# Four-layer attention kernel on one core: the last feed-forward and the final attention placed in other, fewer ticks

## The chip, the core and the metric

The kernel runs on one core of a Trainium2 chip. A core has a matrix engine (TensorE; PE in the profile, its weight loads PEld), a vector engine (VectorE, DVE), a scalar engine for activations (ScalarE, ACT), a general one (GpSimd, POOL) and a sync engine (SP) that issues the DMAs. Each engine works through its own instructions in order; semaphores hold an instruction until what it needs is done. The metric is the device time of one execution in microseconds; the median of several runs counts.

## The reference

`x` is 8 batches of 256 rows by 128, `ctx_512` is 8 batches of 64 rows by 64. Four blocks follow one another:

```python
x = L0(x, ctx_512)      # attention to the context, 16 heads, gate, layer norm
x = L1(x, ctx_512)      # attention to the context, one head, residual
x = L2(ctx_512, x, ...) # six decoder layers: self attention, cross attention, feed-forward
x = L3(x, ctx_512)      # the final attention
```

One decoder layer of L2, and L3, where the change lies:

```python
def step(t, p):
    tn = _ln(t, norm_g, norm_b)
    t = _mha(tn, tn, skv, sq, sow, sob, tgt_mask) + t      # 16 heads of 64
    tn = _ln(t, norm_g, norm_b)
    t = _mha(src, tn, ckv, cq, cow, cob, src_mask) + t
    tn = _ln(t, pg, pb)
    return t + (relu(tn @ w1 + b1) @ w2 + b2)              # 128 -> 512 -> 128

def L3(emb, latent, Wq, bq, Wk, bk, Wv, bv, gamma, beta):
    q = emb @ Wq + bq
    k, v = latent @ Wk + bk, latent @ Wv + bv
    w = softmax(q @ k.T / sqrt(128), axis=1)               # over the 256 rows, not the 64 keys
    x = w @ v + emb
    return layernorm(x, eps=1e-6) * gamma + beta
```

The softmax of L3 runs over the 256 rows of `emb`. The kernel holds the weights with the 64 keys on the partitions, sums along the row, and so can divide the 64 rows of `v` by the sums instead of the weights.

## The kernel before

All activations stay on chip in the tile `t`, 128 rows by 16 blocks by 128 (two blocks a batch). The work is cut into steps of one batch (or half a batch), and every step is put into a table by hand: `at(tick, phase, fn)`. At the end the table is walked tick by tick, and within a tick by phase; each step's instructions are chained behind those before them on the same engine (PE, DVE, ACT, POOL; SP's queue follows the order in which the DMAs are issued). So the table alone sets each engine's order. A tick has no length of its own: it is only the place of a step in the queues, and a step that waits holds everything behind it on that engine.

In the rest of the text, ticks are counted from the first cross-attention tick of the last layer (`T_ca` of layer 5 is tick 0). Batch `b` of the last layer's cross attention has its scores in ticks 2b and 2b+1 (`sc`, L341 and L348, then L357 on ACT, L359 on DVE, L360 on POOL, and L366 on ACT at phase 8), divides a tick later (L370 and L371 on DVE, L372 on POOL), transposes another tick later (L380 on DVE), and sums with the values (L388 on PE, phase 3.0, and L1104 on DVE) in ticks 2b+3 and 2b+4. The last scores stand in tick 15 and the last sums in tick 18. The values of the cross attention (L303) and, for every second batch, its keys (L1079) are made in even ticks.

`plan_ff` places the feed-forward of a batch: the statistics of the normalisation (`moments`, L808 and L809 on DVE; `scales`, L814 to L821 on POOL), the normalisation (L827, ACT), its transpose (L841 on PE, L843 on ACT), `first` (L1120 on PE, L1125 Relu on ACT, the residual L290 on POOL) and `second` (L1137 on PE, L1141 on DVE, which writes `t`).

`plan_l3` places the final attention in five steps, one a tick:

- `trans`: two transposes of `t` (L1158, PE) and a copy (L1160, ACT).
- `project`: queries and values (L1164, L1165 on PE; L1169, L1173 on DVE).
- `weights`: scores (L1177, PE), maximum (L1179, DVE), exponential with its sum (L1182, ACT).
- `values`: reciprocal of the sum (L1186, DVE) and scaling of `v` (L1187, DVE), the product (L1190, PE), the residual (L1195, DVE), the statistics (L262, L263 on DVE; L265, L267 on POOL).
- `finish`: the normalisation (L1201, DVE), scale and shift (L1205, L1206 on POOL) and the store (L1207, SP).

`keys_l3` makes the keys of all batches of L3 once (L407 on PE, L416 on DVE). Its tile shares its place (tag `AT`, one buffer) with the folded keys of the layer before, which are read last in tick 10.

The steps of the last layer in ticks, with the phase in brackets:

| step | batches 0 to 5 | batch 6 | batch 7 |
|---|---|---|---|
| moments, scales | 2b+4 (6, 8.4) | 16 (6, 8.4) | 18 (6, 8.4) |
| normalisation | 2b+5 (3.3) | 17 (3.3) | 19 (3.3) |
| its transpose | 2b+6 (2.9) | 18 (2.9) | 20 (2.9) |
| first | 2b+7 (3.1) | 19 (3.1) | 21 (3.1) |
| second | 2b+8 (3.2) | 20 (3.2) | 22 (3.2) |
| trans | 2b+9 (4.5) | 21 (4.5) | 23 (4.5) |
| project | 2b+10 (4.4) | 22 (4.4) | 24 (4.4) |
| weights | 2b+11 (4.3) | 23 (4.3) | 25 (4.3) |
| values | 2b+12 (4.2) | 24 (4.2) | 26 (4.2) |
| finish | 2b+13 (4.1) | 25 (4.1) | 27 (4.1) |

The keys of L3 are made in tick 11 (3.9).

Of the kernel before, what the change touches and what calls it, by code (L numbers as in the profile page):

```python
# [12 lines left out]
ALU = mybir.AluOpType  # L13
# [4 lines left out]
B, S, D = 8, 256, 128  # L18
M, DM = 64, 64
NL, H, HD, FF = 6, 16, 64, 512  # L20
# [7 lines left out]
def tile_xattn_stack(ctx: ExitStack, tc: tile.TileContext, io, out: bass.AP):  # L28
    nc = tc.nc
# [31 lines left out]
    def sb(shape, tag, bufs=2, pool=None):  # L61
        return (pool or act).tile(shape, F32, tag=tag, name=uniq(tag), bufs=bufs)
# [216 lines left out]
    def at(tick, phase, fn):  # L279
        plan.setdefault(tick, []).append((phase, fn))  # L280
# [121 lines left out]
    S0 = {}  # L402
# [399 lines left out]
    def ahead(b, stats_at, normal_at, tT_at, g, bias, st, on_scalar=True):  # L802

        def moments():
            st["mv"] = sm([P, QT, 2], "mv")
            for j in range(QT):
                six = sm([P, 6], "six")
                nc.vector.bn_stats(six, tt(b)[:, j, :])  # L808
                nc.vector.bn_aggr(st["mv"][:, j, :], six)  # L809

        def scales():
            mv = st["mv"]
            ve = sm([P, QT], "ve")
            nc.gpsimd.tensor_scalar(ve, mv[:, :, 1], 1e-5, None, ALU.add)  # L814
            st["rstd"] = sm([P, QT], "rstd")
            nc.gpsimd.tensor_tensor(st["rstd"], ve, mhalf, ALU.pow)
            if on_scalar:
                nm = sm([P, QT], "nm")
                nc.gpsimd.tensor_tensor(nm, mv[:, :, 0], st["rstd"], ALU.mult)
                st["nm"] = sm([P, QT], "nm2")  # L820
                nc.gpsimd.tensor_scalar(st["nm"], nm, -1.0, None, ALU.mult)  # L821

        def normal():
            st["xn"] = sb([P, QT, D], "xn", 3)
            for j in range(QT):
                if on_scalar:
                    nc.scalar.activation(  # L827
                        st["xn"][:, j, :], tt(b)[:, j, :], AF.Identity,
                        scale=st["rstd"][:, j : j + 1], bias=st["nm"][:, j : j + 1],
                    )  # L830
                else:
                    nc.vector.tensor_scalar(
                        st["xn"][:, j, :], tt(b)[:, j, :], st["mv"][:, j, 0:1],
                        st["rstd"][:, j : j + 1], ALU.subtract, ALU.mult,
                    )

        def trans():
            ps = tp_tile()
            xn = st.pop("xn")
            for j in range(QT):  # L840
                nc.tensor.transpose(ps[:, j * P : (j + 1) * P], xn[:, j, :], ident)  # L841
            st["tT"] = sb([D, S], "tT", 5)
            nc.scalar.activation(st["tT"], ps[:, :S], AF.Identity, scale=g, bias=bias)  # L843

        at(*stats_at, moments)
        at(stats_at[0], 8.4, scales)
        at(*normal_at, normal)
        at(*tT_at, trans)
# [260 lines left out]
                nm2[:, b].unsqueeze(1).to_broadcast([P, 4, M]), lambda ps, qt=qt: add(qt, ps),  # L1109
            )  # L1110

    def plan_ff(l, b, T, T_second):
        st = {}

        def first():
            w1 = W["ff", l][0]
            hT = big("o", shape=(P, FF // P, S))
            ps = two_banks("mm")
            for c in range(FF // P):
                nc.tensor.matmul(  # L1120
                    ps[:, c * S : (c + 1) * S], lhsT=w1[:, c * P : (c + 1) * P], rhs=st["tT"],
                    start=True, stop=True,
                )
            for c in range(FF // P):
                nc.scalar.activation(  # L1125
                    hT[:, c, :], ps[:, c * S : (c + 1) * S], AF.Relu, bias=ff_b1[:, l, c : c + 1]
                )
            st["hT"] = hT
            st["tb"] = residual(b, W["ff", l][2])

        def second():
            w2 = W["ff", l][1]
            ps = mm_tile()
            hT = st.pop("hT")
            for j in range(QT):
                for c in range(FF // P):
                    nc.tensor.matmul(  # L1137
                        ps[:, j * D : (j + 1) * D], lhsT=hT[:, c, j * P : (j + 1) * P],
                        rhs=w2[:, c, :], start=(c == 0), stop=(c == FF // P - 1),
                    )  # L1140
            nc.vector.tensor_add(  # L1141
                tt(b), ps[:, :S].rearrange("p (a d) -> p a d", a=QT), st["tb"]
            )

        ahead(b, (T - 3, 6), (T - 2, 3.3), (T - 1, 2.9), pre_g[:, l : l + 1], pre_b[:, l : l + 1], st)
        at(T, 3.1, first)
        at(T_second, 3.2, second)

    out_v = out.rearrange("b (j p) d -> b p j d", p=P)
# [1 line left out]
    def plan_l3(b, T):  # L1151

        st = {}

        def trans():
            ps = tp_tile()
            for j in range(QT):
                nc.tensor.transpose(ps[:, j * P : (j + 1) * P], tt(b)[:, j, :], ident)  # L1158
            st["tT"] = sb([D, S], "tT", 5)
            nc.scalar.copy(st["tT"], ps[:, :S])  # L1160

        def project():
            ps = mm_tile()
            nc.tensor.matmul(ps[:, :S], lhsT=w3q, rhs=st.pop("tT"), start=True, stop=True)  # L1164
            nc.tensor.matmul(  # L1165
                ps[:M, S : S + D], lhsT=ctx2[:DM, b], rhs=w3v, start=True, stop=True
            )
            st["q"] = sb([D, S], "q1")
            nc.vector.tensor_scalar(  # L1169
                st["q"], ps[:, :S], b3q, float(D) ** -0.5, ALU.add, ALU.mult  # L1170
            )
            st["v"] = sb([M, D], "v1")
            nc.vector.tensor_add(st["v"], ps[:M, S : S + D], b3v)  # L1173

        def weights():
            sc = mm_tile()
            nc.tensor.matmul(sc[:M, :S], lhsT=S0["k3T"][:, b], rhs=st.pop("q"), start=True, stop=True)  # L1177
            nm = sm([M, 1], "nm3")
            nc.vector.tensor_reduce(nm, sc[:M, :S], AX.X, ALU.max, negate=True)  # L1179
            st["e"] = sb([M, S], "tT", 5)  # L1180
            st["rs"] = sm([M, 1], "rs3")
            nc.scalar.activation(st["e"], sc[:M, :S], AF.Exp, bias=nm, accum_out=st["rs"])  # L1182

        def values():
            v, rs = st.pop("v"), st.pop("rs")
            nc.vector.reciprocal(rs, rs)  # L1186
            nc.vector.tensor_scalar(v, v, rs, None, ALU.mult)  # L1187
            ps = mm_tile()
            for j in range(QT):
                nc.tensor.matmul(  # L1190
                    ps[:, j * D : (j + 1) * D], lhsT=st["e"][:, j * P : (j + 1) * P], rhs=v,
                    start=True, stop=True,
                )
            y = st["y"] = sb([P, QT, D], "y")
            nc.vector.tensor_add(y, ps[:, :S].rearrange("p (a d) -> p a d", a=QT), tt(b))  # L1195
            st["norm"] = stats(y, 1e-6)

        def finish():
            y, (mv, rstd) = st.pop("y"), st.pop("norm")
            for j in range(QT):  # L1200
                nc.vector.tensor_scalar(  # L1201
                    y[:, j, :], y[:, j, :], mv[:, j, 0:1], rstd[:, j : j + 1],
                    ALU.subtract, ALU.mult,
                )
            nc.gpsimd.tensor_tensor(y, y, ln3_g.unsqueeze(1).to_broadcast([P, QT, D]), ALU.mult)  # L1205
            nc.gpsimd.tensor_tensor(y, y, ln3_b.unsqueeze(1).to_broadcast([P, QT, D]), ALU.add)  # L1206
            nc.sync.dma_start(out=out_v[b], in_=y)  # L1207

        for n, step in enumerate((trans, project, weights, values, finish)):
            at(T + n, 4.5 - 0.1 * n, step)  # L1210


    at(0, -1, lambda: load_sa(0))
# [3 lines left out]
    for b in range(B):  # L1217
        plan_l0(b, 2 * b)
        plan_l1(b, 2 * b + 7)
    T0 = 2 * B + 1  # L1220
    for l in range(NL):
        T_ca = T0 + 4 * B
        T_next = T_ca + 2 * B
        for b in range(B):
            plan_sa(l, b, T0 + 4 * b)
        plan_ca_weights(l, T_ca - 6)
        for b in range(B):
            plan_ca(l, b, T_ca + 2 * b)
            T_ff = T_ca + 2 * b + 7
            plan_ff(l, b, T_ff, T_ff + (2 if l + 1 < NL else 1))  # L1230
        if l > 0:
            at(T0 + 8, -1, lambda l=l: load_ff(l))
        if l + 1 < NL:
            at(T_ca + 4, -1, lambda l=l: load_sa(l + 1))
            at(T_next + 1, -1, lambda l=l: load_ca(l + 1))
        T0 = T_next
    def keys_l3():
        S0["k3T"] = sb([D, B, M], "AT", 1, heap)
        keys(w3k, S0["k3T"], b3k)

    at(T_ca + 11, 3.9, keys_l3)
    for b in range(B):
        plan_l3(b, T_ca + 2 * b + 9)

    engines = (
        mybir.EngineType.PE, mybir.EngineType.DVE, mybir.EngineType.Activation,
# [72 lines left out]
```

## Time and profile before

| | |
|---|---|
| median of 3 runs | 2443.6 us (2442.93 to 2445.48) |
| the profiled execution's own time | 2442.87 us |
| its span in the profile | 2441.1 us |
| granted clock of PE, mean of the span | 0.987 |
| busy share of the span | PE 96%, PEld 71%, DVE 75%, ACT 70%, POOL 59% |
| chain that ended last | PE 77%, DVE 8%, ACT 7%, POOL 5%, issue 2% |
| start of L388 in ticks 11 to 18 (us from the span's start) | 2331.7, 2341.4, 2351.2, 2359.2, 2373.6, 2379.9, 2388.9, 2397.7 |

The span runs from the first to the last event of the profile; the execution's own time holds 1.8 us more. "Busy" is the time in which an engine has an instruction in work. The timeline gives an instruction's start, its duration, and in brackets how long the engine was idle before it and what ended that. "A <- B: 5.3, 3, 2.4" in the list of waits reads: A waited for B, 5.3 us in all, three times, 2.4 us the longest. The windows view gives for each stretch its length, then the busy time of each engine with the number of instructions, the granted clock of PE, the DMA share and GB/s. Times in the text are from the span's start.

### The profile page before, as it was taken

The numbers are of one execution on the slowest core, as the hardware profiler recorded it, in microseconds if no ns is written. First come the engines' busy times: TensorE is split into PE (matmuls) and PEld (weight loads), VectorE is DVE, ScalarE is ACT, GpSimd is POOL, SyncE is SP. The second block draws the span as 40 slices with busy tenths as digits, with TensorE's granted clock in tenths as the row PEclk, the third lists the DMA queues.
The fourth block names the chain that finished last, engine by engine and source line by source line (L and its number), as shares of the span: only waits on it lengthen the run. The fifth ranks groups of instructions, "written<-read, shape, count | busy, mean of one in ns | idle before, by whom it ended". The sixth has DMA issues, their size and how long they took to land.

```text
span 2441.1 us, 99984 instructions
## 1 busy us (share of the span) xinstructions
PE 2349.7 (96%) x42411; PEld 1742.3 (71%) x42411; DVE 1839.3 (75%) x5988; ACT 1718.1 (70%) x4528; POOL 1450.2 (59%) x2483
## 2 busy tenths in 40 slices
PE   8999999999999999999999999999999999999986
PEld 4667777777777677777777777777777777777764
DVE  5778887677887667887767887667888667888664
ACT  5577777677777667777667777667777667778642
POOL 4845557754556755556855556755556765555763
PEclk9999999999999999999999999999999999999998
DMA  6000022000022001022001022001012000010000
GB/s 177 2 11 14 23 75 57 2 12 21 20 72 64 2 3 30 20 72 64 2 3 30 20 63 64 11 3 30 20 55 72 12 2 26 24 53 5 2 3 16
DMA packets 102833, 76.88 MB, mean 31 GB/s; under 512 B 8113, under 2 KB 96881, under 8 KB 102386
## 3 DMA queue, kind: packets, MB, share of 16 engines
q1 hardware_dynamic: 101794, 70.16, 10.4%
q8 instruction: 334, 5.47, 0.9%
q14 instruction: 113, 0.93, 0.1%
q10 hardware_dynamic: 592, 0.33, 0.1%
HBM read 62.07 MB, written 8.39 MB: 29 GB/s over the span
## 4 chain that ended last, share of the span: by engine, by line
PE 77%; DVE 8%; ACT 7%; POOL 5%; issue 2%; DMA 0%; SPq 0%; POOLq 0%; DVEq 0%; ACTq 0%
PE mm L861 14%; PE sc L898 14%; PE mm L953 13%; PE mm L971 7%; PE mm L880 7%; PE mm L388 5%; PE sc L341 4%; PE mm L1120 3%; PE mm L1137 2%; DVE m L359 2%; ACT e L357 2%; POOL e L360 2%; PE mm L1079 2%; PE tp L841 1%; PE mm L303 1%
## 5 line engine op out<-in xcount | busy, mean ns | idle before, releaser
L927 POOL TENSOR_SCALAR e<-e,rs 128x256 f32<-128x256 f32 x1536 | 703.0, 478 | 673.3 <-DVE rs L925 664.0
L917 ACT ACTIVATE e<-e,mn 128x256 f32<-128x256 f32 x1536 | 758.2, 495 | 133.8 <-DVE mn L912 129.5
L912 DVE CUSTOM_DVE_ANT_0 e<-sc,nm 128x256 f32<-128x256 f32 x1536 | 542.4, 419 | 107.7 <-PE sc L898 106.2
L937 DVE STREAM_TRANSPOSE eTc<-e 128x512 f32<-128x512 f32 x768 | 517.3, 695 | 62.5 <-POOL e L927 61.2
L898 PE MATMUL sc<-k,q 64*32 64x256 f32 x12288 | 377.7, 380 | 1.9 <-ACT v L286 1.0
L953 PE MATMUL mm<-eTc,v 32*64 32x256 f32 x12288 | 363.9, 377 | 5.7 <-ACT AT L1054 3.3
L953 PEld LDWEIGHTS mm<-eTc,v 32*64 32x64 f32 x12288 | 277.3, 131 | 88.7 <-issue 22.7
L359 DVE TENSOR_REDUCE m<-sc 128x16 f32<-128x1024 f32 x112 | 136.7, 1221 | 269.2 <-ACT e L357 269.2
L360 POOL TENSOR_TENSOR e<-e,m 128x1024 f32<-128x1024 f32 x112 | 213.1, 1902 | 209.8 <-DVE m L359 209.8
L898 PEld LDWEIGHTS sc<-k,q 64*32 64x32 f32 x12288 | 221.3, 106 | 122.2 <-issue 48.9
L917 ACT ACTIVATION_READ_ACCUMULATOR e<-e,mn 128x1 f32 x1536 | 287.1, 187 | 0.0
L341 PE MATMUL sc<-q,tT 128*32 128x256 f32 x3072 | 222.0, 388 | 3.0 <-DVE t L1104 2.3
L372 POOL TENSOR_TENSOR e<-e,r 128x1024 f32<-128x1024 f32 x112 | 213.0, 1902 | 2.9 <-DVE r L371 2.9
L388 PE MATMUL mm<-v,o 128*128 128x128 f32 x1536 | 202.2, 287 | 0.0
L388 PEld LDWEIGHTS mm<-v,o 128*128 128x128 f32 x1536 | 188.9, 201 | 16.1 <-issue 8.7
L861 PE MATMUL mm<-tT,w_sk 128*128 128x256 f32 x768 | 189.1, 389 | 0.0
L971 PEld LDWEIGHTS mm<-w_sow,o 128*128 128x128 f32 x1536 | 175.1, 192 | 17.0 <-issue 12.3
L880 PE MATMUL mm<-w_sv,tT 128*32 128x256 f32 x3072 | 185.7, 382 | 0.0
L286 ACT COPY v<-mm 128x1024 f32<-128x1024 f32 x96 | 97.2, 1012 | 124.3 <-PE mm L880 123.7
L971 PE MATMUL mm<-w_sow,o 128*128 128x128 f32 x1536 | 183.6, 278 | 0.8 <-ACT WVO L1052 0.8
L861 PE MATMUL mm<-tT,w_sq 128*128 128x256 f32 x768 | 173.6, 379 | 0.0
L861 PEld LDWEIGHTS mm<-tT,w_sk 128*128 128x128 f32 x768 | 138.1, 190 | 44.1 <-issue 29.2
(212 smaller groups left out, 3544.5 us busy)
## 6 DMA issues: line engine op xcount, KB each, us to landing
nm<-mask_d SPq DMA_DIRECT2D x192, 128.0 KB
wd<-o SPq DMA_DIRECT2D x48, 128.0 KB
w_sk<-in_L_sa_kv_dram SPq DMA_DIRECT2D x6, 512.0 KB
w_sv<-in_L_sa_kv_dram SPq DMA_DIRECT2D x24, 128.0 KB
w_sq<-in_L_sa_q_dram SPq DMA_DIRECT2D x6, 512.0 KB
w_sow<-in_L_sa_ow_dram SPq DMA_DIRECT2D x6, 512.0 KB
w_ckv<-in_L_ca_kv_dram SPq DMA_DIRECT2D x12, 256.0 KB
w_cq<-in_L_ca_q_dram SPq DMA_DIRECT2D x6, 512.0 KB
```

Of the source, the lines that this page charges most:

```text
L341: nc.tensor.matmul(sc[32 * a : 32 * a + 32, q, :], lhsT=qT()[:, qb * 32 : (qb + 1) * 32], rhs=keys()[:, a].rearrange("p h k -> p (h k)"), ...
L360: nc.gpsimd.tensor_tensor(e, e, m.unsqueeze(2).to_broadcast([P, 16, M]), ALU.subtract)
L388: nc.tensor.matmul(ps[:, :D], lhsT=eT[:, s].rearrange("p q x -> p (q x)"), rhs=vw[:, r, k, g, :], start=(s == 0), stop=(s == 7),)
L861: nc.tensor.matmul(ps[:, i * S : (i + 1) * S], lhsT=w[:, c * P : (c + 1) * P], rhs=st["tT"], start=True, stop=True,)
L880: nc.tensor.matmul(ps[32 * a : 32 * a + 32, i, :], lhsT=st["tT"][:, kb * 32 : (kb + 1) * 32], rhs=sv[:, a].rearrange("p g x -> p (g x)"), ...
L898: nc.tensor.matmul(sc[32 * a : 32 * a + 32, r, j, :], lhsT=st["q"][g][rows, a, qb * 32 : (qb + 1) * 32], rhs=st["k"][g][rows, a, :], start ...
L912: nc.vector.tensor_tensor_reduce(e[:, i, :], sc4[:, i, :], st["nm"][:, 2 * jj + i % 2, :], -1.0, 3.0 * BIG, ALU.add, ALU.min, mn[:, i : i ...
L917: nc.scalar.activation(e[:, i, :], e[:, i, :], AF.Exp, scale=-1.0, bias=mn[:, i : i + 1], accum_out=rs[:, i : i + 1],)
L927: nc.gpsimd.tensor_scalar(e[:, i, :], e[:, i, :], rs[:, i : i + 1], 1.0, ALU.mult, ALU.mult)
L937: nc.vector.transpose(eT[:, r, :, 2 * jj : 2 * jj + 2, :], e[:, 2 * r : 2 * r + 2, :].rearrange("p j (k x) -> p k j x", x=32),)
L953: nc.tensor.matmul(ops[a // 2][r * HD : (r + 1) * HD, a % 2, :S], lhsT=st["v"][kb // 4][rows, kb % 4, (2 * g + r) * HD : (2 * g + r + 1) * ...
L971: nc.tensor.matmul(st["ps"][:, j * D : (j + 1) * D], lhsT=st["oT"][c // 4][:, c % 4, j * P : (j + 1) * P], rhs=sow[:, c, :], start=(c == 0 ...
```

## The change

Three things are moved; no instruction is added or left out.

- The feed-forward of the last layer for batches 6 and 7 takes other ticks.
- The final attention begins in the tick behind `second` at phase 0.5, that is at the tick's head; `project` follows in the same tick at 4.5, `weights` one tick later, and the division of `v` becomes a step of its own at the end of that tick (8.6); `values` and `finish` follow one and two ticks behind.
- The keys of L3 are made in tick 6 instead of 11, in a buffer of the ring `k`, which the cross attention of the last layer does not use.

The new places:

| step | batches 0 to 5 | batch 6 | batch 7 |
|---|---|---|---|
| moments, scales | 2b+4 (6, 8.4) | 16 (6, 8.4) | 18 (6, 8.4) |
| normalisation | 2b+5 (3.3) | 16 (8.7) | 18 (8.7) |
| its transpose | 2b+6 (2.9) | 18 (2.9) | 19 (2.9) |
| first | 2b+7 (3.1) | 18 (4.6) | 19 (4.6) |
| second | 2b+8 (3.2) | 19 (3.2) | 20 (3.2) |
| trans, project | 2b+9 (0.5, 4.5) | 20 (0.5, 4.5) | 21 (0.5, 4.5) |
| weights, divide | 2b+10 (4.3, 8.6) | 21 (4.3, 8.6) | 22 (4.3, 8.6) |
| values | 2b+11 (4.2) | 22 (4.2) | 23 (4.2) |
| finish | 2b+12 (4.1) | 23 (4.1) | 24 (4.1) |

The diff, cut to its core:

```diff
-    def plan_ff(l, b, T, T_second):
+    def plan_ff(l, b, T, T_second, steps=None):
...
-        ahead(b, (T - 3, 6), (T - 2, 3.3), (T - 1, 2.9), pre_g[:, l : l + 1], pre_b[:, l : l + 1], st)
-        at(T, 3.1, first)
+        first_at, *steps = steps or (3.1, (T - 3, 6), (T - 2, 3.3), (T - 1, 2.9))
+        ahead(b, *steps, pre_g[:, l : l + 1], pre_b[:, l : l + 1], st)
+        at(T, first_at, first)
         at(T_second, 3.2, second)
...
+        def divide():
+            rs = st.pop("rs")
+            nc.vector.reciprocal(rs, rs)
+            nc.vector.tensor_scalar(st["v"], st["v"], rs, None, ALU.mult)
+
         def values():
-            v, rs = st.pop("v"), st.pop("rs")
-            nc.vector.reciprocal(rs, rs)
-            nc.vector.tensor_scalar(v, v, rs, None, ALU.mult)
+            v = st.pop("v")
...
-        for n, step in enumerate((trans, project, weights, values, finish)):
-            at(T + n, 4.5 - 0.1 * n, step)
+        at(T, 0.5, trans)
+        at(T, 4.5, project)
+        at(T + 1, 4.3, weights)
+        at(T + 1, 8.6, divide)
+        at(T + 2, 4.2, values)
+        at(T + 3, 4.1, finish)
...
-            plan_ff(l, b, T_ff, T_ff + (2 if l + 1 < NL else 1))
+            if l + 1 < NL:
+                plan_ff(l, b, T_ff, T_ff + 2)
+            elif b < B - 2:
+                plan_ff(l, b, T_ff, T_ff + 1)
+            else:
+                T_ff -= b - B + 3
+                done = T_ca + 2 * b + 4
+                plan_ff(
+                    l, b, T_ff, T_ff + 1,
+                    (4.6, (done, 6), (done, 8.7), (T_ff, 2.9)),
+                )
+            T_end[b] = T_ff + 1
...
-        S0["k3T"] = sb([D, B, M], "AT", 1, heap)
+        S0["k3T"] = big("k", shape=(D, B, 2 * M))[:, :, :M]
         keys(w3k, S0["k3T"], b3k)
 
-    at(T_ca + 11, 3.9, keys_l3)
+    at(T_ca + 6, 3.9, keys_l3)
     for b in range(B):
-        plan_l3(b, T_ca + 2 * b + 9)
+        plan_l3(b, T_end[b] + 1)
```

From `plan_l3` on the changed file has other line numbers (the copy L1160 is L1161 there, the product L1190 is L1194, the normalisation L1201 is L1205); the prediction names lines by the numbers of before.

More of the change, by code (lines that the diff above doesn't have):

```diff
@@ L1220, in tile_xattn_stack @@
     T0 = 2 * B + 1
+    T_end = {}
     for l in range(NL):
```

## The prediction

> **What bounds the kernel now.** I read the page first, then windows and PE's waits over the last 110 us, the chain of waits there, and the timeline. PE is busy 96% of the span and carries 77% of the chain, so time is won only where PE stands or runs slowly, and behind its last large group. The windows view of the stretch that the change touches:
>
> ```profile
> 2341.36:2359.17 17.81, 16.00 (x201) 11.59 (x199) 13.76 (x29) 7.52 (x15) 12.05 (x14) 1.00 0.01 2
> 2359.17:2379.91 20.74, 17.17 (x152) 11.57 (x151) 12.92 (x28) 7.78 (x13) 11.23 (x13) 0.84 0.02 7
> 2397.67:2441.10 43.43, 25.75 (x133) 17.84 (x132) 17.90 (x65) 8.06 (x26) 14.54 (x26) 0.81 0.05 16
> ```
>
> Stretch, length, busy time of PE, PEld, DVE, ACT, POOL, granted clock. Two ticks take 17.8 us with PE busy 16.0, or 20.7 at clock 0.84; behind the last sums (L388, 2397.67) PE is busy 25.75 of 43.4 us. PE's waits from 2331 to 2398, and after 2397.67 (us in all, times, longest):
>
> ```profile
> PE mm L1190 <- DVE v L1187: 5.3, 3, 2.4
> PE tp L841 <- ACT xn L827: 2.2, 2, 1.1
> PE mm L1177 <- DVE AT L416: 1.1, 1, 1.1
> PE sc L341 <- ACT o L1125: 0.7, 1, 0.7
> ...
> PE mm L1190 <- DVE v L1187: 7.3, 5, 2.1
> ```
>
> The first row is the wait for the division: step values stands ahead of the next tick's scores in PE's order, and its L1187 is last in DVE's, behind L1141. The chain of waits (start, us) shows why DVE is late there:
>
> ```profile
> 2356.28 1.87 DVE y L1201 x2
> 2358.15 0.34 DVE nm L1179
> 2358.51 0.56 ACT tT L1182 x2
> 2359.07 0.26 ACT tT L1160
> 2359.33 0.96 ACT e L366
> ...
> 2365.18 0.33 DVE t L1141
> 2365.61 0.76 DVE v L1187
> 2366.41 1.02 PE mm L1190 x4
> ```
>
> In the odd tick output, softmax and copy of the last attention stand ahead of L366, 3.0 us that come out at L1190. What follows such a wait, in windows of 3.41 us:
>
> ```profile
> 2363.26:2366.67 3.41, 0.98 (x34) 0.44 (x16) 3.02 (x8) 1.97 (x2) 3.02 (x2) 1.00 0.00 0
> 2366.67:2370.08 3.41, 3.41 (x20) 1.72 (x23) 2.11 (x8) 0.00 (x0) 1.08 (x3) 0.50 0.00 0
> 2383.74:2387.15 3.41, 1.59 (x37) 0.90 (x24) 2.54 (x8) 1.01 (x1) 1.90 (x1) 1.00 0.00 0
> 2387.15:2390.56 3.41, 3.41 (x13) 2.43 (x13) 2.79 (x12) 0.00 (x0) 1.64 (x4) 0.50 0.00 0
> ```
>
> After PE was busy 0.98 or 1.59 of 3.41 us the clock is 0.50, both times for two windows; at it L388 took 3.78 us (2388.85) against 1.95 (2397.67).
>
> **Part 1: the ticks up to the last sums (2331.7 to 2397.7).** I count ticks from the last layer's first cross-attention tick; L388 of tick 18 starts at 2397.67.
>
> Removed: PE's four waits above, 9.3 us. The first goes because the division now ends a tick (8.6), one tick before values: DVE does it (0.14 and 0.28 to 0.75 us) ahead of L359, which alone is queued behind it and waits 1.1 to 4.0 us for L357 in odd ticks anyway; without that cover it costs its 0.9 a batch, on DVE. The third goes since the keys are built five ticks early; their 1.1 us of PE and 0.7 of DVE move, at nothing (bounds -1.1 and +1.1). The other two are waits of the next tick's first matmuls for ACT (Relu L1125, then the normalisation L827 behind it). Before them PE did weights and trans at the end of an odd tick (0.95 us); now it does values and project there (0.6 + 1.0), 0.65 more cover: the 0.7 becomes 0.1, the 1.1 before L841 becomes 0.4 in tick 16; in tick 18 it goes, since batch 6 is now normalised at the end of tick 16.
>
> Added: trans is now first in a tick (0.5), ahead of all scores, and needs L1141 of the tick before. L1141 ended 0.2 us after L303 at 2346, 1.5 at 2365.5, 1.2 at 2385.9. Weights (0.6) now lies between, and the 3.0 us above leave the odd tick, so I take 0 there and 0.14 of issue each, 0.4; tick 9, with neither, adds 0.9 (L303 ends 2312.1, L1141 2312.9). No row shows the new order: bounds 0 and 2.4 each (the longest L1190 wait). With the 0.5 left above, 1.8 stay. Project and values of one batch more are done by the last sums: +1.6. So -9.3 + 1.8 + 1.6 = -5.9.
>
> Clock: without windows half empty the slow stretches go. L1190, L1164, L1165 and the scores took 2.7 + 4.4 us from 2366.4, against 1.6 (from 2347.2) and 2.3 (from 2356.6): 3.2. L1164, L1165, L388, L1120 took 7.9 from 2387.1, against 1.0 + 1.8 + 1.8: 3.3. Together -6.5.
>
> At nothing, with their cover: POOL's four ops of an output (2.4 us) and its store come a tick sooner; POOL is busy 12.05 of 17.8, and SP's queue holds only such stores then. The two L1201 (1.95 us beside a POOL op, 0.6 alone) and L1179 go to even ticks, where the next tick's first user of DVE's late results is L388, behind scores. L1160 moves ahead of L357 on ACT: 0.25 us, ACT being busy 7.5 of 17.8. If this cover fails each costs its length once a batch.
>
> On the clock the Trainium skill speaks against this change. "TensorE: Matmul & The Clock Gate", section "Why this matters for your kernels", asks only that PE not idle over about 3 us between bursts. By it waits of 2.4 us cost no clock, and their removal wins none. The trace disagrees: 2.4 and 1.8 us idle, and the clock fell.
>
> **Part 2: the drain (2397.67 to 2441.1, 43.4 us).** Of batches 6 and 7 the feed-forward's first product moves from ticks 19 and 21 to 18 and 19, the second from 20 and 22 to 19 and 20; the last attention ends in tick 24 instead of 27. PE's new order from the last sums, at full-clock durations (L388, L1137, L1120 1.8; L1177, L1190 0.6; L1164 with L1165 1.0; trans 0.4): L388, L1137 of batch 5, weights of 4, L1120 of 6, trans of 5: 6.4. Then L841 of batch 7 needs its statistics, whose POOL part stands behind output 3 and a residual: L1201 done 5.0, L1205 and L1206 1.5, L290 0.7, L814 to L821 1.5, L827 to L841 0.6 (timeline): 9.3, a new wait of 2.9 with all of PE behind it. L841, L1137 of 6, values of 4, project of 5, L1120 of 7, trans of 6 end at 15.2; L1137 of 7 waits 0.3 for Relu and ends at 17.3. Three softmaxes follow one another, each 3.1 from L1177 to L1190 (2423.51 to 2426.64), with L1190 between: 17.3 + 3.1 + 0.6 + 3.1 + 0.6 + 3.1 + 0.7 = 28.5. From L1190's end (2433.48) to the span's end: 7.6, so 36.1. Output 7 uses the buffer of output 5, stored at about 26 and landed within 2.9 (last issue 2438.24 to the span's end): 0 to 0.8, I take 0.4. So 36.5 against 43.4: -6.9.
>
> New clock losses: the 2.9 us wait can empty a window, 3.3 as above; the softmaxes leave PE mostly idle, and a second fall costs like that at 2404 (L1120 3.6 against 1.8): 1.7. I take both, +5.0 (bounds 0 and 8.3).
>
> **Sum.** -5.9 - 6.5 - 6.9 + 5.0 = -14.3. The profiled execution took 2442.87 (span 2441.1 and 1.8 around it), 0.7 under the median 2443.6: 2429.3, so 2429.
>
> **Rivals.**
>
> The falls have another cause than the waits. They come as often as before: no 6.5, no 5.0, and the 1.8 at 2404 stays: -5.9 - 6.9 + 1.8 = -11.0, 2432.6. For it: the fall at 2404 came behind a window with PE busy 2.36 of 3.41 us. Against: the two costly ones came behind 0.98 and 1.59. The Trainium skill's rule above would lead here.
>
> Small waits suffice. After 2400.80 PE was busy 2.36 of 3.41 us, and 0.50 followed; so the waits at trans keep the 6.5: -5.9 - 6.9 + 5.0 = -7.8, 2435.8. Against: 2.27 and 2.35 (2407.63, 2411.04) were not followed by it.
>
> The ticks are bound by the loop scores, L357, L359 to L1104 (8 us), whatever PE waits for. DVE's 13.8 of 17.8 speak for it, the 14 us of two earlier ticks (L388 at 2300.5 and 2314.4) against. Then -6.9 + 5.0 = -1.9, 2441.7, no change.
>
> Slower: trans at the tick's head, six times (ticks 9 to 19), has all scores behind it. It decides when L1141 ends later than 0.6 + 1.7 us after L303, half a window empty: six waits of 1.7 are 10.2, a fall in every second pair 9.9, less 1.3 counted, and the 6.5 not won: -14.3 + 18.8 + 6.5 = +11.0, 2454.6. Against: 0.2 to 1.5 us in the rows.
>
> That it does not do what it says: the plan chains each engine's instructions by tick and phase, so only a buffer could hold a step, and those are counted.
>
> **How the numbers follow.** Forecast 0.62, other cause 0.13, small waits 0.14, loop 0.05, slower 0.06. Low end: without new clock losses, trans waits and the keys' 1.1, -14.3 - 5.0 - 1.3 - 1.1 = -21.7, 2421. High end: 2435.8 and one trans wait at its bound, 2438. Outside lie the last two rivals and some of the forecast's tails. 0.2% of the median is 4.9 us, about what a measurement of this kernel can tell from no change. Faster by more: 0.89; within: 0.05; slower: 0.06.
>
> **What would show it.** Right: no PE wait for the division in ticks 12 to 17, waits of trans for L1141 under 1 us, granted clock 1.00 until the last sums, these near 2385; nearly 3 us of wait before the last L841; 36 to 42 us from the last sums to the end. Wrong: clock 0.50 in those ticks (the clock rivals), trans waiting over 1.7 us (slower), last sums after 2392 with PE idle elsewhere (loop).

## The result, and the profile after

The changed kernel takes 2433.9 us (median of 5 runs, 2430.0 to 2435.6) against 2444.7 for the kernel before beside it (5 runs): ratio 0.9953, 95% interval 0.9938 to 0.9967, so the medians lie 10.8 us apart, and the ratio says 0.47%, with an interval from 8 to 15 us. The forecast of 2429 was 4.9 us too low; the range held the time.

The profiled execution of after has a span of 2431.9 us. Its start-up and the layers ahead, where both programs are the same, came out 6.4 us later than in the profile of before, so whole spans mislead here. I compare one stretch instead: from the first L388 of tick 6 (2291.87 before, 2298.24 after) to the end of the span. It took 149.3 us before (the expectations say 149.0) and 133.7 after, 15.6 less, where the forecast's sum was 14.3.

The windows view of after, the columns being stretch, length, busy time of PE, PEld, DVE, ACT, POOL, granted clock, DMA share and GB/s: ticks 12 and 13, ticks 14 and 15, and from the last sums to the end.

```profile
2347.89:2363.84 15.95, 15.92 (x200) 11.61 (x199) 12.64 (x29) 8.68 (x17) 12.61 (x14) 1.00 0.04 10
2363.84:2378.14 14.30, 13.84 (x152) 10.30 (x151) 11.81 (x26) 7.55 (x15) 10.96 (x12) 1.00 0.04 10
2389.69:2431.94 42.25, 26.98 (x126) 19.74 (x124) 15.75 (x59) 8.25 (x23) 14.57 (x26) 0.72 0.05 16
```

In the ticks PE is busy 15.92 of 15.95 us and 13.84 of 14.30, at full clock; before, the same two pairs took 17.81 and 20.74. Behind the last sums nearly nothing changed: 42.25 us for 43.43, at a clock of 0.72 for 0.81. PE's waits from 2300 to 2432 (us in all, times, longest):

```profile
PE mm L1194 <- DVE v L1188: 4.4, 3, 2.0
PE tp L841 <- ACT xn L827: 3.3, 2, 2.9
PE tp L1159 <- DVE t L1141: 0.8, 1, 0.8
PE mm L407 <- DVE t L1104: 0.5, 1, 0.5
...
```

The three waits for the division (L1194) all lie behind the last sums; none is left in the ticks. The row of trans (L1159) is the 0.8 us of tick 9, that of L407 a wait of the keys in their new tick, which the prediction had at nothing. The 2.9 of L841 is the new wait in the drain, and this is what follows it, on PE's timeline and in windows of 3.41 us:

```profile
2395.76 0.38 PE L1159 MATMUL tp<-ident,t 128*128 128x128 f32 x2
2399.02 0.86 PE L841 MATMUL tp<-ident,xn 128*128 128x128 f32 x2 [2.88 <-ACT xn L827]
2399.68 3.62 PE L1137 MATMUL mm<-w_f,o 128*128 128x128 f32 x16
```

```profile
2394.77:2398.18 3.41, 1.37 (x8) 0.96 (x6) 1.28 (x7) 2.13 (x6) 3.03 (x6) 1.00 0.13 38
2398.18:2401.59 3.41, 2.57 (x11) 2.37 (x12) 0.00 (x0) 1.70 (x4) 0.23 (x1) 0.50 0.00 0
2401.59:2405.01 3.42, 3.42 (x14) 2.83 (x13) 0.92 (x3) 0.00 (x0) 0.00 (x0) 0.50 0.00 0
2405.01:2408.42 3.41, 3.41 (x9) 2.13 (x8) 1.44 (x6) 0.00 (x0) 1.61 (x3) 0.50 0.00 0
```

PE was busy 1.37 of 3.41 us, and then three windows ran at 0.50. The chain of waits shows why L841 was late (start, us):

```profile
2393.53 0.42 DVE t L1141
2393.96 0.52 DVE y L1205 x2
...
2394.55 0.73 POOL y L1209
...
2395.35 0.72 POOL y L1210
2396.08 0.68 POOL tb L290
...
2397.14 0.72 POOL rstd L816
...
2398.48 0.50 ACT xn L827
```

It is the chain that the prediction named: output 3 and a residual on GpSimd ahead of batch 7's statistics.

### The profile page after: what moved, and what is told of

The parts are those of the page before. It is cut to its first block, busy times and chain, and to the rows that moved or that the text cites. A ratio compares the mean times of both kernels' runs of the same rounds, so it can differ in the third digit from the quotient of the medians.

```text
span 2431.9 us, 99981 instructions
## 1 busy us (share of the span) xinstructions
PE 2349.5 (97%) x42411; PEld 1741.0 (72%) x42411; DVE 1836.6 (76%) x5988; ACT 1719.9 (71%) x4528; POOL 1450.3 (60%) x2483
## 4 chain that ended last, share of the span: by engine, by line
PE 79%; DVE 7%; ACT 7%; POOL 5%; issue 2%; DMA 0%; SPq 0%; POOLq 0%; DVEq 0%; ACTq 0%
PE mm L861 14%; PE sc L898 14%; PE mm L953 13%; PE mm L971 7%; PE mm L880 7%; PE mm L388 5%; PE sc L341 4%; PE mm L1137 3%; PE mm L1120 3%; DVE m L359 2%; ACT e L357 2%; POOL e L360 2%; PE mm L303 1%; PE tp L841 1%; PE mm L1079 1%
## 5 line engine op out<-in xcount | busy, mean ns | idle before, releaser
L917 ACT ACTIVATE e<-e,mn 128x256 f32<-128x256 f32 x1536 | 758.2, 495 | 133.7 <-DVE mn L912 129.4
L388 PE MATMUL mm<-v,o 128*128 128x128 f32 x1536 | 199.3, 285 | 0.2 <-ACT v L309 0.2
L388 PEld LDWEIGHTS mm<-v,o 128*128 128x128 f32 x1536 | 185.6, 198 | 15.9 <-issue 8.1
```

Source lines behind the costliest of these rows:

```text
L388: nc.tensor.matmul(ps[:, :D], lhsT=eT[:, s].rearrange("p q x -> p (q x)"), rhs=vw[:, r, k, g, :], start=(s == 0), stop=(s == 7),)
L917: nc.scalar.activation(e[:, i, :], e[:, i, :], AF.Exp, scale=-1.0, bias=mn[:, i : i + 1], accum_out=rs[:, i : i + 1],)
```

## The experiments

Three theories were put against each other. Waits: PE is the bound, and its waits for the division with the half clock behind them are what was won. Fewer ticks: the shorter pipeline wins it, and the division is of no account. Another cause: the clock falls have nothing to do with the waits. "Stretch" is always from L388 of tick 6 to the end of the span.

**The division alone.** The kernel before with:

```diff
-        def values():
-            v, rs = st.pop("v"), st.pop("rs")
+        def divide():
+            rs = st.pop("rs")
             nc.vector.reciprocal(rs, rs)
-            nc.vector.tensor_scalar(v, v, rs, None, ALU.mult)
+            nc.vector.tensor_scalar(st["v"], st["v"], rs, None, ALU.mult)
+
+        def values():
+            v = st.pop("v")
...
+        at(T + 2, 8.6, divide)
```

> The kernel before, and of the change only the division taken out of values and put at the end of the same tick as weights (T+2 in the old counting, phase 8.6); every other step keeps its tick. Measure: from the start of L388 in tick 6 to the end of the span (149.0 us before, 133.7 after), and the median. Waits theory (PE's waits for the division, and the half clock behind them, are what the change won in the ticks): the waits of 2.4, 1.8 and 1.1 us in ticks 12 to 17 go (5.3), the clock falls at 2366 and 2387 with them (6.5), and nothing in the drain: the stretch 137 to 139 us, the median 10 to 12 below before. Rival, fewer ticks (the shorter pipeline alone wins it): 148 to 149 us, the same time as before. Rival, the clock falls for another cause: the waits go and the falls stay, 143 to 144 us, 5 below before.

Measured: stretch 133.7 us, ratio 0.9956 (0.9940 to 0.9972). Fewer ticks falls: with no step but the division in another tick the kernel is as fast as after. The stretch is 3 us below even the waits theory's figure, a miss: the drain took 39.4 us for 43.5, where nothing was expected of it.

**Everything but the moved feed-forward.** The kernel after, with `elif True:` in place of `elif b < B - 2:`, so that batches 6 and 7 keep their ticks 2b+7 and 2b+8.

> The kernel after, with the feed-forward of batches 6 and 7 in its old ticks (2b+7 and 2b+8); the final attention's new steps, its division at a tick's end and the early keys stay. Waits theory: up to the last sums as after (ticks 11 to 18 about 50 us), less work ahead of them moved; the drain loses what the move won there, some 4 to 6 us by the two ticks more of dependent steps: the stretch 137 to 140 us, 4 to 6 above after. Rival, fewer ticks: the drain takes back all of it, 146 us or more. A third outcome: the wait of 2.88 us before the last L841 and the 10.2 us of half clock behind it, which the move brought, go with it and pay for the two ticks: 133 to 135 us, as after.

Measured: stretch 128.4 us, median 2426.9, ratio 0.9925 (0.9906 to 0.9944). Ticks 11 to 18 took 50.8 us, as the waits theory has it, but the stretch is none of the three outcomes: without the moved feed-forward the kernel is 5.3 us faster in it. With the division moved, the new places of the attention's steps and the early keys are worth 133.7 - 128.4 = 5.3 over the division alone, and the moved feed-forward gives that back. PE's timeline behind the last sums of this kernel:

```profile
2400.17 0.71 PE L841 MATMUL tp<-ident,xn 128*128 128x128 f32 x2 [0.38 <-ACT xn L827]
2400.72 1.95 PE L1137 MATMUL mm<-w_f,o 128*128 128x128 f32 x16
2402.60 0.65 PE L1178 MATMUL mm<-q,k 128*64 128x256 f32 x2
2403.25 0.44 PE L1159 MATMUL tp<-ident,t 128*128 128x128 f32 x2
2403.53 1.89 PE L1120 MATMUL mm<-tT,w_f 128*128 128x256 f32 x8
2405.54 0.68 PE L1194 MATMUL mm<-v,tT 64*128 64x128 f32 x4
```

Each later batch's feed-forward (L1120, L1137) lies beside an earlier batch's softmax (L1178 to L1194), L841 waits 0.38 us, and the clock is at 1.00 from 2303 to 2412. The drain takes 35.7 us, against 42.3 with the move.

**The moved feed-forward alone.** The kernel before, with the new `plan_ff` calls for batches 6 and 7 and the attention beginning one tick behind; its five steps keep their old phases, the division is inside values, and the keys stay in tick 11.

> The kernel before, with only the feed-forward of batches 6 and 7 moved as in the change and the final attention beginning in the tick behind it; the division stays inside values, trans at its old phase, the keys where they were. Waits theory: the three waits for the division and the falls at 2366 and 2387 stay in ticks 12 to 17, the drain shortens by at most what it did in after, and new division waits lie in it: the stretch 143 to 149 us, the median 0 to 6 below before. Rival, fewer ticks: most of the gain, 134 to 137 us.

Measured: stretch 149.8 us, just outside the 143 to 149 expected, ratio 1.0023 (1.0009 to 1.0037). No gain, a loss if anything: PE's wait for the division is 14.2 us in 8 waits (12.7 before), and the drain took 46.5 us.

**After once more.**

> The kernel after once more, unchanged, beside the others on the same chip. Both theories: the stretch 133 to 135 us, the median 10 to 11 below before. What it tells apart: in the profiled execution of after, L388 of tick 6 stood 6.2 us later than before, with the same instructions up to there. If that comes from the execution (where the clock falls in the start-up), it lies anywhere from -7 to +7 here; if it comes from the changed program, it is 6 to 7 again, and the change's gain in the last stretch is larger than the medians show, with a cost ahead of it that the prediction did not have.

Measured: stretch 133.8 us, ratio 0.9957 (0.9942 to 0.9972), and waits equal to the tenth. L388 of tick 6 at 2294.29, 4 us earlier than in the first profile of the same program: the start-up differs between executions, the stretch did not.

**The division back into values.** The kernel after with:

```diff
-        def divide():
-            rs = st.pop("rs")
-            nc.vector.reciprocal(rs, rs)
-            nc.vector.tensor_scalar(st["v"], st["v"], rs, None, ALU.mult)
-
         def values():
-            v = st.pop("v")
+            v, rs = st.pop("v"), st.pop("rs")
+            nc.vector.reciprocal(rs, rs)
+            nc.vector.tensor_scalar(v, v, rs, None, ALU.mult)
...
-        at(T + 1, 8.6, divide)
```

> The kernel after, with the division put back into values (at its head, tick T+2, phase 4.2); every other new place stays. In the trace of after, VectorE comes to that place in an odd tick behind L1104 (2340.59 in the repeated run), while PE reached the product L1194 at 2339.42: the division would end near 2341.3, so L1194 would wait some 1.9 us in each of the ticks 11, 13, 15 and 17. Waits theory: 4 x 1.9 = 7.6 us of waits, and 3 to 7 us of half clock behind them: the stretch from L388 of tick 6 to the end 141 to 149 us (133.7 with the division moved), the median 7 to 15 above after. Rival, the places of the other steps are what counts: 133 to 136 us, within 2 of after.

Measured: stretch 146.5 us, median 2447.5, ratio to before 1.0007 (0.9998 to 1.0016): the whole gain is gone, though every other new place stays; the new places pay only together with the division. PE's waits in the ticks, 2325 to 2398 (L1191 is the product, L1188 the division in this kernel):

```profile
PE mm L1191 <- DVE v L1188: 8.3, 3, 2.9
```

Three waits of 2.8 us where four of 1.9 were expected, and three clock falls of 3.4 us each (2343, 2363, 2384) at them; ticks 11 to 18 took 62.3 us, for 50.0 in after.

**Something to do while waiting.** The kernel before with, at the head of values' product:

```diff
+            fill = two_banks("fill")
+            for n in range(8):
+                nc.tensor.matmul(
+                    fill[:, :P], lhsT=ident, rhs=ident, start=True, stop=True
+                )
```

> The kernel before, with eight idle 128x128 matmuls (identity by identity, into a PSUM tile that nobody reads) ahead of the product of values in each batch: PE has something to do while it waits for the division, and the wait itself stays. It adds work and leaves none out. If the half clock follows a window of 3.41 us in which PE was mostly idle: the falls at 2366 and 2387 go though the division comes as late as before, the ticks 11 to 18 take 58 to 61 us against 65.9, the stretch 141 to 144 us. If the falls have another cause: they stay, and the matmuls cost 0 to 3 us: ticks 11 to 18 take 66 to 69 us, the stretch 149 to 152.

PE's timeline at the place of the 2.4 us wait (L1188 is the idle matmuls, L1195 the product):

```profile
2373.01 1.09 PE L303 MATMUL mm<-WVO,ctx 64*32 64x256 f32 x32
2374.04 2.05 PE L1188 MATMUL fill<-ident 128*128 128x128 f32 x16
2376.53 0.71 PE L1195 MATMUL mm<-v,tT 64*128 64x128 f32 x4 [0.44 <-DVE v L1192]
2377.17 0.70 PE L1164 MATMUL mm<-tT,L_Wq 128*128 128x256 f32 x2
```

The product of values still begins 2.4 us behind the end of L303, but the clock stays at 1.00 up to 2434, and L1164 takes 0.70 us. Ticks 11 to 18 took 60.5 us (58 to 61 expected), the stretch 145.0 (141 to 144 expected: the drain took 44.6 us for 43.5). So the falls come from PE's idling, not from something else at that place, if this execution was not merely one in which they would have stayed out; the grid below settles that. As a kernel it wins nothing: ratio 1.0013 (0.9999 to 1.0026).

**Before once more, twice**, the second time also timed against itself.

> The kernel before once more, with a profile. In five profiled executions of changed kernels L388 of tick 6 stood 2.4 to 9.6 us later than in the one profile of before, with the same instructions up to there, and all five had a clock fall near 40 us that it lacked. If this is chance in where the 3.41 us windows of the clock lie, before has it here too: L388 of tick 6 at 2294 to 2299 instead of 2291.9, and with the medians unchanged a stretch behind it of 143 to 147 us. If it belongs to the changed programs, it stands at 2291 to 2293 again and the stretch at 149.

> The kernel before once more, timed as the others are, against itself. In the traces the stretch from L388 of tick 6 to the end differs between kernels by 4 to 5 us more than the medians do (after: 133.7 against 149.3, 15.6, where the medians give 10.8). If this comes from how the runs were taken, the ratio here is 1.001 to 1.003 (2.5 to 7 us over the runs beside it) with the same program. If it comes from the changed programs, the ratio is 1.000 within its interval.

The first gave L388 of tick 6 at 2299.61 and a stretch of 149.3 us: the start-up moved by 7.7 us in the same program, the stretch by nothing. That is neither outcome whole: the start as if by chance, the stretch as if not. The second was timed at a ratio of 1.0003 (0.9989 to 1.0016): no difference that can be told. Its stretch, however, was 140.7 us, with the same waits of PE (12.6 us at L1190) and no clock fall in the ticks at all. Windows of that execution around the 2.43 us wait, which lay from 2369.7 to 2372.1:

```profile
2367.57:2370.99 3.42, 2.15 (x43) 1.43 (x41) 3.38 (x7) 1.16 (x2) 2.73 (x2) 1.00 0.00 0
2370.99:2374.40 3.41, 2.25 (x24) 1.44 (x28) 2.47 (x9) 0.81 (x1) 1.08 (x2) 1.00 0.00 0
```

and of the other, where the wait of 2.42 us lay inside one window:

```profile
2370.97:2374.38 3.41, 0.98 (x34) 0.44 (x17) 3.04 (x8) 1.97 (x2) 3.03 (x2) 1.00 0.00 0
2374.38:2377.79 3.41, 3.41 (x20) 1.72 (x23) 2.08 (x8) 0.00 (x0) 1.05 (x3) 0.50 0.00 0
```

In these executions the same wait cost half-clock time or none, and what differs is where the clock's windows lie against the program. They lie on a grid of 3.41 us within an execution and elsewhere in the next: the falls of the first two profiles of before lie on a grid 0.8 us behind L388 of tick 11, those of the third 2.9 behind it. Laying such a grid over PE's busy time of the third execution at 17 positions 0.2 us apart, 12 have a window with PE busy under 1.7 us around the waits, and 5 (2.4 to 3.2) have none. Of the 12, nine have such a window at both the 2.4 and the 1.8 us wait, three at the first alone. The same over the ticks of the kernel with the division alone, and of the one with the idle matmuls: none at any position. By this measure neither owes its full clock to a lucky position; and the idle matmuls' execution had its grid 0.9 us behind L388 of tick 11, where before has both falls. Over after, around its wait of 2.88 us: 15 of 17.

The 1.7 us is no sharp border. In the thirteen profiles, from 2285 us on, every window at full clock with PE busy under 1.65 us was followed by half clock; of those between 1.69 and 2.4 us some were (2.36 us, at 2404, in the first profile of before) and most were not. One more fall shifts the stretches a little: eight of the thirteen profiles have one of a single window at L388 of tick 6, the stretch's start, and take 0.4 to 0.7 us longer from there to tick 7 than the same order without it. It lies in the two stretches of 149.3 us and in every stretch below 130, not in 140.7 or in those of 133.7 and 133.8.

**Batch 7's statistics early.** The kernel after, with moments, scales and normalisation of batch 7's feed-forward at phases 3.15 to 3.17 of tick 18:

```diff
-        at(stats_at[0], 8.4, scales)
+        at(stats_at[0], 3.16 if stats_at[1] == 3.15 else 8.4, scales)
...
+                    (4.6, (done, 3.15), (done, 3.17), (T_ff, 2.9)) if b == B - 1 else
                     (4.6, (done, 6), (done, 8.7), (T_ff, 2.9)),
```

> The kernel after, with the statistics and the normalisation of batch 7's feed-forward (moments, scales, normalisation) straight behind its sums in tick 18 (phases 3.15 to 3.17), ahead of the output of batch 3 in the queues of VectorE and GpSimd. Theory: the moved feed-forward costs what it does (the division's move and the new places without it took 128.4 us, with it 133.7) by the wait of 2.88 us before the last L841 and the 10.2 us of half clock behind it. Then the wait falls below 1 us, the fall at 2398 goes with it, and the stretch comes to 126 to 129 us, the median 5 to 8 below after. Rival: the cost is that three softmaxes follow one another at the end with no feed-forward beside them (waits of 0.97, 1.44 and 1.96 us before L1194, then half clock to the end); then only the 2.9 us go: 130 to 132 us.

Measured: stretch 126.9 us, median 2428.2, ratio 0.9929 (0.9909 to 0.9949). PE's timeline at the place:

```profile
2398.79 0.38 PE L1159 MATMUL tp<-ident,t 128*128 128x128 f32 x2
2399.01 0.38 PE L841 MATMUL tp<-ident,xn 128*128 128x128 f32 x2
2399.57 2.47 PE L1137 MATMUL mm<-w_f,o 128*128 128x128 f32 x16 [0.19 <-ACT o L1125]
```

The wait and the three slow windows are gone. From L841 to the next L1178 PE needs 9.56 us (2399.01 to 2408.57), where the repeated run of after needed 13.26 (2395.08 to 2408.34): 3.7 us of clock and 2.88 of wait are 6.6 of the 42.3 - 35.0 = 7.3 us that the drain lost. The same grid over this kernel's drain around L841 has no window under 1.7 us at any position. The rival falls, though three softmaxes still follow one another.

**Weights of batches 6 and 7 early, besides** (`at(T + 1, 4.15 if b >= B - 2 else 4.3, weights)`).

> The kernel with batch 7's statistics early (stretch 126.9 us), and besides the weights of batches 6 and 7 at phase 4.15 in place of 4.3, ahead of the values of the batch before. In that kernel's end each L1178 stands behind the L1194 for whose division PE waits (0.94, 1.44, 2.43 us), so the three softmaxes follow one another. Theory: a score product that does not wait for the division of the batch before begins its softmax about 1 us sooner; two of them: the stretch 124 to 126 us. Rival: VectorE's queue sets the pace (L1180 stands there behind the sums and statistics of the batch before), and PE's order changes nothing: 126.5 to 127.5 us.

Measured: stretch 126.5 us, median 2424.4, ratio 0.9920 (0.9892 to 0.9947). PE's waits at L1194 fell from 4.8 us in three to 1.9 in one, and the stretch by 0.4: the rival's figure. The chain of waits at the end of this run shows which queue it is:

```profile
2408.42 0.61 DVE y L1205 x2
...
2409.10 0.73 POOL y L1209
...
2409.90 0.72 POOL y L1210
...
2411.47 0.22 POOL ve L265
...
2411.77 0.72 POOL rstd L267
```

The normalisation of one output, two passes on GpSimd, and there the next batch's scale behind them: 4.1 us a batch (2408.42 to the next L1205 at 2412.51). PE is no longer the bound there.

**Batch 7's attention beside batch 6's.** The kernel with the early statistics, and besides weights of batch 6 at 4.15, output 7 written over its own input, and batch 7's steps thus:

```diff
+            at(T, 4.18, project)
+            at(T, 4.19, weights)
+            at(T, 8.7, divide)
+            at(T + 1, 4.25, values)
+            at(T + 2, 4.15, finish)
```

> The kernel with batch 7's statistics early (126.9 us), and the last attention of batch 7 drawn together with that of batch 6: its projection and weights in the tick of batch 6's weights (phases 4.18 and 4.19, ahead of the values of batch 5), its division behind batch 6's, its values behind batch 6's values; output 7 is written over its own input, so that it does not wait for the store of output 5. Theory: the three softmaxes overlap, and the chain from the first of them to the last L1194 shortens from 8.6 us (2411.5 to 2420.1) to 5 or 6: the stretch 123 to 125 us. Rival, VectorE and GpSimd hold the chain (two sums, statistics and outputs are then queued behind one another): 126 to 128 us, no gain over the kernel with the early statistics.

Measured: stretch 127.1 us, median 2429.1, ratio 0.9936 (0.9915 to 0.9957). No gain, as the rival said. The three kernels with early statistics are not told apart by their intervals, and neither is the one without the moved feed-forward (0.9906 to 0.9944) from them. The lowest median, that with the weights early, is 20.0 us under that of before beside it, after's repeat 10.5 under its own, and it is the one that I would keep. That the moved feed-forward with early statistics beats leaving it where it was is not shown.

## Why the prediction was right, and where it was not

**The waits: right.** From tick 6 to the last sums, full clock in both, the third run of before and after in windows:

```profile
2298.16:2396.99 98.83, 88.37 (x1077) 65.82 (x1075) 66.35 (x149) 54.29 (x98) 68.56 (x82) 1.00 0.02 4
2298.24:2389.69 91.45, 89.14 (x1085) 66.67 (x1083) 65.52 (x155) 54.69 (x100) 68.74 (x82) 1.00 0.02 6
```

Before took 98.83 us with PE busy 88.37, after 91.45 with 89.14. PE stands 8.2 us less (7.5 forecast: 9.3 removed, 1.8 added) and works 0.8 more (1.6 forecast): -7.4 against -5.9. Trans waited 0.8 us in tick 9 and nowhere else, so what the small waits and the slower rival needed did not come; ticks 11 to 18, down from 59.5 us without falls to 50.0, refute the loop's bound.

**The clock in the ticks: right in size, wrong in how often.** 65.9 us for ticks 11 to 18 with the falls and 59.5 without them, 6.4 (6.5 forecast). But the prediction counted it in full, as if every execution of before had it. Three profiles of before gave stretches of 149.3, 149.3 and 140.7; of the 8.6 us between them 6.4 lie in ticks 11 to 18, 1.6 in the drain and 0.6 at tick 6. Of the grid's 17 positions nine have both falls in the ticks and three one. An estimate from that, if every position is as likely: 6.4 x 9/17 + 3.2 x 3/17 = 4.0, so before's mean stretch is 144.7 us, or up to 146.9 with the other 2.2 in full, and the gain 11.0 to 13.2 where one profile against the other gives 15.6; the median's 10.8 (8 to 15) agrees. Of the 4.9 us by which 2429 was too low, 1.1 is that before's median came out at 2444.7 for 2443.6, and nearly all the rest is the gain, 10.8 for 14.3. The step behind it, as far as these runs tell, is this one: a median was set equal to one execution, which had the falls in its ticks, and so a slow stretch, and an early start (2291.87, against 2298.16 and 2299.61 in the two others), the one hiding the other. How much the start-up adds to single comparisons I can't say from these runs beyond that spread.

That the sum of 14.3 lies near the 15.6 of that one pair of profiles is in part luck: the ticks gave 7.4 for 5.9, the clock in them 6.4 for 6.5, the drain 1.2 for 1.9, and tick 6 0.6 that no term had.

The measured 10.8 is near the figure of the rival "another cause" (11.0), so the time alone could not tell the two apart. Its mechanism is refuted all the same: idle matmuls in the wait remove the falls, and the early statistics do so in the drain. The Trainium skill's rule on idle gaps, "TensorE: Matmul & The Clock Gate", section "Why this matters for your kernels", would have a wait of 2.4 us cost nothing; two executions of before contradict it and the third, where two windows share the wait, looks as if it held.

**The drain: right in sum, wrong in its reason.** Forecast 36.5 us at full clock and 5.0 of clock loss, 41.5; measured 42.3. The wait before L841 was 2.88 (2.9 forecast), each softmax 3.0 to 3.1 from L1178 to L1194 (3.1), from the last L1194's end to the span's end 7.7 (7.6). The losses were the two that the prediction took, one fall of three windows behind the wait and half clock under the last softmaxes. The comparison with the early statistics gives 4.4 us besides the wait, 3.7 of it by the first fall (3.3 forecast); that kernel has half clock at its end too, so what the second cost (1.7 forecast) is not shown. What failed is the reason for the term -6.9, the two moved products and the shorter pipeline together. The prediction priced the new order against before and never the order without the move: that one takes 35.7 us, so the division and the new places of the attention bring 7.8 (43.5 to 35.7; 6.2 from the third run's 41.9), and the move takes 6.6 back, for 0.8 us won in ticks 11 to 18 (50.8 to 50.0). The drain's sum came out near the measured time although one of its parts gained and the other lost.

**The change's parts in the stretch,** from the runs: before 149.3 or 140.7; division alone 133.7; new places and keys besides 128.4; the moved feed-forward besides, which is after, 133.7; early statistics besides 126.9. Of the 7.0 us between 140.7 and 133.7, 4.5 lie in ticks 11 to 18 (59.54 to 55.06), where the three waits of 2.4, 1.8 and 1.1 us went and 0.9 before L1164 came, and 2.5 in the drain (41.9 to 39.4), where the division's waits fell from five to two.

## What to carry to other kernels

Price each part of a change against the change without it, not only against the kernel before: here one part gave back what another had won, and the sum hid it. When a wait empties PE, price the clock behind it by its chance over the positions of the clock's windows, and compare stretches that lie behind the same instructions rather than whole spans. Work brought forward in one engine's order costs time when what it waits for is not brought forward too.

## What was not expected of the hardware

One and the same 2.4 us wait of PE was followed by 6.8 us at half clock in two executions and by none in a third. What separates them, as far as these profiles show, is how the 3.41 us windows cut it: PE busy 0.98 us in one of them, or 2.15 and 2.25 in two. After a window with PE busy 1.37 us the half clock lasted three windows, although PE was busy 2.57, 3.42 and 3.41 us in them; in before it lasted two behind 0.98 and 1.59, and with the division back in values one behind each of the three waits. What sets that length stays open.
